# Two attention layers on one core: value products for 512 queries, output products in one step behind the value transposes

## The chip, the core and the metric

The kernel runs on one core of a Trainium2 chip. The metric is the device time of one execution in microseconds; for each kernel the median of several runs is given. The profile is that of one execution, taken by the hardware profiler; its times are in microseconds unless marked ns. Its engines are PE (TensorE's matmuls), PEld (TensorE's weight loads), DVE (VectorE), ACT (ScalarE), POOL (GpSimd) and SP (SyncE, which here issues most DMAs).

## The reference

Two layers of the same form run over an input of 4 images of 32 x 32 positions and 768 channels, all in float32. Each layer adds to its input an attention over the group-normalised input. With 12 heads of 64 channels and 1024 positions:

```python
qkv = x @ Wqkv                                   # layer 1 also adds a bias
q, k, v = ...                                    # (B * 12, 1024, 64) each
rel_h = jnp.einsum('bhwc,hkc->bhwk', r_q, Rh)    # relative positions, rows
rel_w = jnp.einsum('bhwc,wkc->bhwk', r_q, Rw)    # and columns
bias = rel_h[..., :, None] + rel_w[..., None, :]
scores = scale * jnp.einsum('bqc,bkc->bqk', q, k) + bias
attn = jax.nn.softmax(scores, axis=-1)
out = jnp.einsum('bqk,bkc->bqc', attn, v)
return out @ Wproj + bproj
```

## The kernel before

**Units of work.** The 2 layers x 4 images are 8 images in a row. The 12 heads of an image are taken in 6 pairs, one head on partitions 0 to 63 and the other on 64 to 127, so there are 48 pairs, `g`. The 1024 queries of a pair are taken in 8 tiles of 128. One `(g, n)` is a unit, and the main loop (line 520) makes one step for each. The eight steps of a pair are called a slot below, its steps 0 to 7.

**What a step does**, in the order in which it is written. The order on each engine is the order of the program. `run(early)` issues what earlier steps put off: DMAs, relative positions, statistics. What a function puts into `early` runs in the next step, what it puts into `later` runs two steps on (one step on, if it was put there while `run(early)` ran). `biases` (two GpSimd additions, line 303) prepares the unit two ahead. `scores` computes the unit one ahead: 4 matmuls on PE (line 315), two DVE reductions that add the bias and take the minimum of the negated scores (line 324), two exps on ACT (line 328). `turn` transposes the present unit's weights on DVE in blocks of 32 (line 352), and for every second unit, that is for each quarter of 256 queries, writes them to memory (`td`, line 355), from where `read_back` (line 361) brings them back as `pt` with the keys on the partitions. `divide` takes reciprocals of the sums on DVE (line 335) and multiplies on GpSimd (line 338). `take(todo, n)` runs n units of pending PE work, `weigh` the product of weights and values.

**Pending PE work.** `todo` holds for each slot six input groups of the next pair (`project_in`, line 222: q, k and v, each in two halves, 6 units of two matmuls each), and behind them four output groups (`project_out`, line 437, usually 3 units of one matmul each) of the image. An input group ends with an ACT copy (lines 232 or 234) and a DVE addition (line 235), an output group with a DVE addition (446 or 449), and in layer 0 with statistics of the new image (line 149). `shares` says how many units each step takes: 6 in every step, as a rule. In steps with an even number, a first output group is taken ahead of `turn`, so that its eviction isn't queued behind the transposes on DVE.

**Values.** When an input group of v is complete, `late` gets `turn_values` (line 247): 8 transposes on PE (line 252) and one ACT copy (line 253). It runs at the end of a step, behind `weigh`. `weigh` (line 366) runs in every even step for one quarter of 256 queries: 16 matmuls (line 373) and a DVE copy (line 378).

**Shapes on the array.** Scores, positions and inputs contract over 64 rows and fill 128 columns, two at a time in the two halves of the array (64*128 in the profile). `weigh` contracts over 128 rows with 64 columns (128*64). Outputs and value transposes use the whole array (128*128).

**Buffers.** PSUM holds two pools of two buffers: `ps_s` for scores, and `ps_m` for all else (inputs, positions, value transposes, value products, outputs), whose two buffers are taken in turn. `tb` has three buffers, `pt` two for each head, `td` two for each head.

**Image boundaries.** The next image is normalised in stages: statistics (`load_stats`, `stats`), exchange over groups of channels (`norm`: gather, by_group, groups, spread, in steps 1, 3, 5, 7 of pair 3), and `apply` for each of six tiles (line 197): three in steps 2 to 4 of pair 4, three in step 0 of pair 5, ahead of the input groups that read them.

Of the kernel before, what the change touches and what calls it, by code (L numbers as in the profile page):

```python
# [31 lines left out]
FP = mybir.dt.float32  # L32
# [4 lines left out]
P = 128  # L37
B, HW, C = 4, 32, 768
S = HW * HW
# [15 lines left out]
def attention_blocks(ctx: ExitStack, tc: tile.TileContext, a: dict, out: bass.AP):  # L55
# [284 lines left out]
    def turn(g, n):  # L340

        quarter, j = divmod(n, 2)
        for h in range(2):
            if j == 0:
                tb_of[h] = tbpool.tile([P, HW, 2, HW], FP, tag="tb", name=f"tb_{g}_{n}_{h}")  # L350
            tb = tb_of[h]
            nc.vector.transpose(tb[:, :, j, :], sc_of[g, n, h])  # L352
            if j == 1:
                td = dram2.tile([P, S * 2], FP, tag=f"td{h}", name=f"td_{g}_{n}_{h}")
                nc.sync.dma_start(out=td, in_=tb.rearrange("p k n i -> p (k n i)"))
                behind.append(lambda queue=None, h=h, td=td: read_back(g, quarter, h, td, queue))

    def read_back(g, quarter, h, td, queue=None):
        pt = ptpool.tile([P, 4, NT, 2 * HW], FP, tag=f"pt{h}", name=f"pt_{g}_{quarter}_{h}")
        pt_of[g, quarter, h] = pt  # L360
        (queue or nc.sync).dma_start(
            out=pt.rearrange("p r k t -> p r (k t)"),
            in_=td.rearrange("(r j) (y t) -> (j y) r t", r=4, y=4),
        )

    def weigh(g, quarter):
        if quarter == 0:
            attn_of[g] = apool.tile([P, S], FP, tag="attn", name=f"attn_{g}")
        av = ps_m.tile([P, S], FP, tag="m", name=f"av_{g}_{quarter}")[:, : 2 * P]
        for k in range(NT):  # L370
            for h in range(2):
                rows = slice(h * D, (h + 1) * D)
                nc.tensor.matmul(  # L373
                    av[rows, :], lhsT=v_of[g][:, k, rows], rhs=pt_of[g, quarter, h][:, :, k, :],
                    start=(k == 0), stop=(k == NT - 1),
                )
        at = quarter * 2 * P
        nc.vector.tensor_copy(  # L378
            attn_of[g][:, at : at + 2 * P].rearrange("p (n r i) -> p r n i", n=2, r=4),
            av.rearrange("p (r n i) -> p r n i", n=2, r=4),  # L380
        )


# [46 lines left out]
    def project_out(im, p, o, i):  # L430
        l, b = images[im]
        rows = slice(o * P, (o + 1) * P)
        cols = slice(i * HALF, (i + 1) * HALF)
        c0, c1 = cuts(im)[p : p + 2]
        t = ps_m.tile([P, S], FP, tag="m", name=f"o_{im}_{p}_{o}_{i}")[:, :HALF]
        for c in range(c0, c1):
            nc.tensor.matmul(  # L437
                t, lhsT=wo_of[im, o, c], rhs=attn_of[im * NP + c][:, cols],
                start=(c == c0), stop=(c == c1 - 1),
            )  # L440
# [12 lines left out]
        if at_end:  # L453
            if p == 2:
                nc.sync.dma_start(out=dst[rows, cols], in_=res)
        else:
            early.append(lambda: nc.sync.dma_start(out=dst[rows, cols], in_=res))
        if i == 1 and p < 2:
            early.append(lambda: fetch(place[im, p, o, i] + 4))
        yield True  # L460

    early, mid, later, late, behind = [], [], [], [], []

    def run(todo):
        while todo:
# [9 lines left out]
    def at_outputs(groups):  # L479

        return groups[0][1] if groups and groups[0][1] <= NC // 2 else 0

    def take(groups, n):

        while groups and n > 0:
            group, count = groups[0]
            if next(group, None) is None:
                groups.pop(0)
            else:
                groups[0] = (group, count - 1)  # L490
                n -= 1
        while groups and groups[0][1] == 0:
            for _ in groups.pop(0)[0]:
                pass

    with tc.manual_schedule(engines=ENGINES):
        for c in range(NC):
            for i in range(2):
                stats(0, c, i, xn_of[0][c][:, i * HALF : (i + 1) * HALF])
        stages, apply = norm(0)  # L500
        for stage in stages:
            stage()
        for c in range(NC):
            apply(c)
        todo = prepare(0)
# [12 lines left out]

        units = [(g, n) for g in range(NPAIR) for n in range(NT)]
        for at, (g, n) in enumerate(units):  # L520
            im, pair = divmod(g, NP)
            end = im + 1 == NI
            if n == 0:
                shares = [NC] * NT
                ins = (todo if at == 0 else []) + (prepare(g + 1) if g + 1 < NPAIR else [])
                if pair < 3:
                    if im == 0:
                        shares = [NC if pair == 0 or n != 2 else 0 for n in range(NT)]
                        shares[6] = 0
                    todo = ins + (put_out(im - 1, 1, range(4 * pair, 4 * pair + 4)) if im else [])  # L530
                elif pair < NP - 1:
                    todo = ins + put_out(im, 0, range(4 * pair - 12, 4 * pair - 8))
                    if pair == 3 and not end:
                        stages, apply = norm(im + 1)
                else:
                    todo = ins + put_out(im, 0, range(8, 12))
                    if end:
                        fetch_last()
                        todo += put_out(im, 1, range(12)) + put_out(im, 2, range(0, 12, 2))
                        shares = [6, 3, 3, 4, 2, 4, 2, 6]  # L540
            if pair < 3 and not end and n % 4 == 0 and 2 * pair + n // 4 < AHEAD:
                load_x(im + 1, 2 * pair + n // 4)
            if pair < 3 and im + 1 < B and n % 2 == 0:
                c, i = divmod(4 * pair + n // 2, 2)
                load_stats(im + 1, (c + AHEAD) % NC, i)
            run(early)
            early, later = later, early
            if at + 2 < len(units):
                biases(*units[at + 2])
            if at + 1 < len(units):  # L550
                scores(*units[at + 1])
            ready = late[:1]
            del late[:1]
            ready_reads = list(behind)
            behind.clear()
            if pair == 3 and n % 2 and not end:
                stages[n // 2]()
            if pair == 4 and n in range(2, 2 + AHEAD) and not end:
                apply(n - 2)
            if pair == NP - 1 and n == 0 and not end:  # L560
                for c in range(AHEAD, NC):
                    apply(c)
            share = shares[n]
            first = min(share, at_outputs(todo)) if n % 2 == 0 else 0
            take(todo, first)
            turn(g, n)
            run(ready_reads)
            if at + 1 < len(units):
                divide(*units[at + 1])
            take(todo, share - first)  # L570
            if n % 2 == 0 and at > 3:
                weigh(units[at - 4][0], units[at - 4][1] // 2)
            run(ready)
        for read in behind:
            read(nc.scalar)
        weigh(NPAIR - 1, 2)
        while todo:
            take(todo, 1)
            run(early)
        weigh(NPAIR - 1, 3)  # L580
        todo = put_out(NI - 1, 2, range(1, 12, 2))
        take(todo, len(todo))

# [46 lines left out]
```

## Time and profile before

| | |
|---|---|
| time, median of 3 runs | 3642.38 us (3632.63 to 3643.9) |
| span of the profiled execution | 3635.1 us |
| granted TensorE clock | 0.997 |
| memory traffic | 1090.59 MB, 300 GB/s in the mean |
| DMA engines, main queue | 81.6% of 16 engines' time |
| write of the weights (`td<-tb`) | 384 of 1024 KB, 7.3 us to landing |
| read of the weights (`pt<-td`) | 384 of 1024 KB, 7.5 us to landing |

How to read it: in the profile's first part each engine has its busy time, its share of the span and the number of its instructions. In its second part the span is cut into 40 slices, and each digit is the busy share (or the granted clock) in tenths. Groups of instructions are named out<-in by the program's tiles, with the line of the kernel, the count and the mean duration. In a timeline the first two numbers are the start and the duration of a run of like instructions; matmuls are pipelined, so the durations of neighbours overlap and the difference of two starts is the time that the first one took. What stands in brackets is idle time of the engine ahead of the instruction, and who ended it.

### The profile page before, as it was taken

The numbers are of one execution on the slowest core, as the hardware profiler recorded it, in microseconds if no ns is written. First come the engines' busy times: TensorE is split into PE (matmuls) and PEld (weight loads), VectorE is DVE, ScalarE is ACT, GpSimd is POOL, SyncE is SP. The second block draws the span as 40 slices with busy tenths as digits, with TensorE's granted clock in tenths as the row PEclk, the third lists the DMA queues.
The fourth block names the chain that finished last, engine by engine and source line by source line (L and its number), as shares of the span: only waits on it lengthen the run. The fifth ranks groups of instructions, "written<-read, shape, count | busy, mean of one in ns | idle before, by whom it ended". The sixth has DMA issues, their size and how long they took to land.

```text
span 3635.1 us, 51496 instructions
## 1 busy us (share of the span) xinstructions
PE 3558.3 (98%) x19200; PEld 1717.1 (47%) x19200; DVE 2380.7 (65%) x3628; ACT 1316.8 (36%) x1992; POOL 2292.4 (63%) x1548
## 2 busy tenths in 40 slices
PE   6999999999999999999999999999999999999998
PEld 3544444444444444444444444444444444444443
DVE  4676666766667666666666666666666666666665
ACT  2344333333333333333333343333333333333331
POOL 3676666666656666666666666666666566666663
PEclk9999999999999999999999999999999999999999
DMA  4888888898888988888888989888888888898888
GB/s 141 298 314 294 313 293 307 297 312 311 293 310 300 312 300 309 316 293 311 307 302 309 313 281 328 303 304 300 300 314 299 311 288 315 297 321 284 304 293 305
DMA packets 632346, 1090.59 MB, mean 300 GB/s; under 512 B 248096, under 2 KB 310304, under 8 KB 582944
## 3 DMA queue, kind: packets, MB, share of 16 engines
q1 hardware_dynamic: 580352, 1034.87, 81.6%
q10 hardware_dynamic: 51744, 52.44, 4.2%
q8 instruction: 151, 2.47, 0.3%
q14 instruction: 99, 0.81, 0.1%
HBM read 583.74 MB, written 503.41 MB: 299 GB/s over the span
## 4 chain that ended last, share of the span: by engine, by line
PE 84%; DMA 9%; DVE 3%; issue 2%; SPq 1%; POOL 1%; ACT 0%; DVEq 0%; POOLq 0%
PE pj L222 36%; PE s L315 17%; PE av L373 17%; PE o L437 11%; DMA td<-tb 4%; PE tp L267 2%; DMA pt<-td 2%; PE vt L252 1%; DVE sc L324 1%; DVE tb L352 1%; POOL sc L338 1%; SPq L293 1%; DMA xs<-in_x 1%; DMA part<-res 1%; DMA w<-in_wqkv 0%
## 5 line engine op out<-in xcount | busy, mean ns | idle before, releaser
L338 POOL TENSOR_SCALAR sc<-sc,sm 128x1024 f32<-128x1024 f32 x768 | 849.3, 1118 | 1246.9 <-DVE sm L335 1215.7
L222 PE MATMUL pj<-xn,w 64*128 64x512 f32 x6912 | 1541.4, 591 | 40.1 <-DVE xn L197 38.0
L303 POOL TENSOR_TENSOR sc<-rel 128x1024 f32<-128x1024 f32 x768 | 1454.0, 1914 | 45.0 <-DMA rel<-tdr 45.0
L328 ACT ACTIVATE sc<-sc,sm 128x1024 f32<-128x1024 f32 x768 | 879.0, 1145 | 1366.4 <-DVE sm L324 1366.4
L324 DVE CUSTOM_DVE_ANT_0 sc<-s,sc 128x1024 f32<-128x1024 f32 x768 | 909.5, 1222 | 479.0 <-PE s L315 403.4
L222 PEld LDWEIGHTS pj<-xn,w 64*128 64x128 f32 x6912 | 673.6, 188 | 858.4 <-issue 799.5
L352 DVE STREAM_TRANSPOSE tb<-sc 128x1024 f32<-128x1024 f32 x768 | 918.6, 1225 | 149.0 <-DMA td<-tb 147.1
L315 PE MATMUL s<-k,q 64*128 64x512 f32 x3072 | 751.4, 605 | 6.2 <-DVE sm L324 6.2
L373 PE MATMUL av<-pt,v 128*64 128x256 f32 x6144 | 715.0, 384 | 12.4 <-DMA pt<-td 12.4
L373 PEld LDWEIGHTS av<-pt,v 128*64 128x64 f32 x6144 | 427.5, 137 | 358.3 <-issue 76.1
L437 PE MATMUL o<-attn,wo 128*128 128x512 f32 x1128 | 510.8, 601 | 4.3 <-DVE sum L449 2.7
L315 PEld LDWEIGHTS s<-k,q 64*128 64x128 f32 x3072 | 276.9, 187 | 316.8 <-issue 267.5
L437 PEld LDWEIGHTS o<-attn,wo 128*128 128x128 f32 x1128 | 206.0, 190 | 301.7 <-issue 291.4
L378 DVE COPY attn<-av 128x256 f32<-128x256 f32 x192 | 80.9, 422 | 283.3 <-PE av L373 283.1
L235 DVE TENSOR_TENSOR v<-pj,v 128x512 f32<-128x512 f32 x96 | 107.5, 1120 | 132.1 <-ACT v L234 70.2
L272 ACT COPY t<-tp 128x1024 f32<-128x1024 f32 x96 | 97.1, 1012 | 206.3 <-PE tp L267 205.3
L253 ACT COPY v<-vt 128x1024 f32<-128x1024 f32 x48 | 48.6, 1012 | 262.0 <-PE vt L252 262.0
L328 ACT ACTIVATION_READ_ACCUMULATOR sc<-sc,sm 128x1 f32 x768 | 143.4, 187 | 0.0
L267 PEld LDWEIGHTS tp<-tab,q 64*128 64x128 f32 x1536 | 97.5, 187 | 47.0 <-issue 38.6
L235 DVE TENSOR_TENSOR q<-pj,q 128x512 f32<-128x512 f32 x96 | 65.7, 685 | 72.7 <-ACT q L232 37.3
L235 DVE TENSOR_TENSOR k<-pj,k 128x512 f32<-128x512 f32 x96 | 65.7, 685 | 71.2 <-ACT k L232 39.9
L267 PE MATMUL tp<-tab,q 64*128 64x128 f32 x1536 | 106.3, 278 | 5.3 <-DVE k L235 5.3
(38 smaller groups left out, 755.3 us busy)
## 6 DMA issues: line engine op xcount, KB each, us to landing
td<-tb SPq DMA_DIRECT2D x384, 1024.0 KB, 7.3
pt<-td SPq DMA_DIRECT2D x382, 1024.0 KB, 7.5
w<-in_wqkv SPq DMA_DIRECT2D x144, 384.0 KB, 8.5
tdr<-t ACTq DMA_DIRECT2D x96, 512.0 KB, 7.5
rel<-tdr SPq DMA_DIRECT2D x768, 32.0 KB, 2.3
part<-res SPq DMA_DIRECT2D x96, 256.0 KB, 8.3
res<-part SPq DMA_DIRECT2D x96, 256.0 KB, 3.2
wo<-in_wo SPq DMA_DIRECT2D x90, 192.0 KB, 7.5
```

The lines of the kernel that those rows point to most:

```text
L222: nc.tensor.matmul(t[:, a, :], lhsT=w[rows, c, :], rhs=xn[c][rows, cols], start=(c == 0), stop=(c == NC - 1),)
L235: nc.vector.tensor_tensor(to, t[1], to, ALU.add)
L267: nc.tensor.matmul(ps[:, h, j, :], lhsT=q[rows, at * P : (at + 1) * P], rhs=tabs[l][rows, :], start=True, stop=True,)
L272: nc.scalar.copy(t, ps.rearrange("p h j r -> p j h r"))
L303: nc.gpsimd.tensor_tensor(sc, rel[:, h, 0, n, :].unsqueeze(2).to_broadcast([P, HW, HW]), rel[:, h, 1, n, :].unsqueeze(1).to_broadcast([P, ...
L315: nc.tensor.matmul(ps[h][:, cols], lhsT=q[rows, n * P : (n + 1) * P], rhs=k[rows, cols], start=True, stop=True,)
L324: nc.vector.tensor_tensor_reduce(out=sc, in0=ps[h], in1=sc, scale=-scale, scalar=BIG, op0=ALU.add, op1=ALU.min, accum_out=st[:, 0, h : h + 1],
L328: nc.scalar.activation(sc, sc, AF.Exp, bias=st[:, 0, h : h + 1], scale=-1.0, accum_out=st[:, 1, h : h + 1],)
L338: nc.gpsimd.tensor_scalar(sc, sc, st[:, 2, h : h + 1], 1.0, ALU.mult, ALU.mult)
L352: nc.vector.transpose(tb[:, :, j, :], sc_of[g, n, h])
L373: nc.tensor.matmul(av[rows, :], lhsT=v_of[g][:, k, rows], rhs=pt_of[g, quarter, h][:, :, k, :], start=(k == 0), stop=(k == NT - 1),)
L437: nc.tensor.matmul(t, lhsT=wo_of[im, o, c], rhs=attn_of[im * NP + c][:, cols], start=(c == c0), stop=(c == c1 - 1),)
```

## The change

The change sorts PE's work by the shape in which it uses the array, so that the shape changes less often in a slot:

- `weigh` takes two quarters at once (512 queries[...]) and runs in step 6 for the first two quarters of the pair, in step 2 of the next slot for the other two. Nothing else but scores (and positions) runs on PE in these steps.
- All four output groups run in step 7, and `turn_values` moves from the end of a step to just ahead of them, right behind the scores of step 7.
- Input groups run in steps 0, 1, 3, 4 (two) and 5.
- The read-back of the first and third quarter is put off by a step (`behind2`), the loads for the output groups too (`later`), the statistics and stages move to other steps, and the next image's tiles are applied in steps 2, 6 and 7 of pair 4, four of them between the first and second output group.
- In the last slot the shares differ, and the last two quarters are weighed one by one.

```diff
-                behind.append(lambda queue=None, h=h, td=td: read_back(g, quarter, h, td, queue))
+                (behind if quarter % 2 else behind2).append(
+                    lambda queue=None, h=h, td=td: read_back(g, quarter, h, td, queue)
+                )
...
-    def weigh(g, quarter):
-        if quarter == 0:
+    def weigh(g, quarters):
+        if quarters[0] == 0:
...
+        for at, quarter in enumerate(quarters):
+            for k in range(NT):
+                for h in range(2):
+                    rows = slice(h * D, (h + 1) * D)
+                    nc.tensor.matmul(
+                        av[rows, at * 2 * P : (at + 1) * 2 * P], lhsT=v_of[g][:, k, rows],
+                        rhs=pt_of[g, quarter, h][:, :, k, :], start=(k == 0), stop=(k == NT - 1),
+                    )
...
-            early.append(lambda: fetch(place[im, p, o, i] + 4))
+            (early if im + 1 == NI else later).append(lambda: fetch(place[im, p, o, i] + 4))
...
-                shares = [NC] * NT
+                shares = [6, 6, 0, 6, 12, 6, 0, 12]
...
-                    if im == 0:
-                        shares = [NC if pair == 0 or n != 2 else 0 for n in range(NT)]
-                        shares[6] = 0
+                    if at == 0:
+                        shares = [12, 6, 0, 6, 12, 6, 0, 0]
...
-                        shares = [6, 3, 3, 4, 2, 4, 2, 6]
+                        shares = [0, 6, 6, 4, 2, 2, 0, 8]
...
-            if pair < 3 and im + 1 < B and n % 2 == 0:
+            if pair < 3 and im + 1 < B and n in (1, 3, 5, 6):
...
             if at + 1 < len(units):
                 scores(*units[at + 1])
-            ready = late[:1]
-            del late[:1]
-            ready_reads = list(behind)
-            behind.clear()
-            if pair == 3 and n % 2 and not end:
-                stages[n // 2]()
-            if pair == 4 and n in range(2, 2 + AHEAD) and not end:
-                apply(n - 2)
-            if pair == NP - 1 and n == 0 and not end:
-                for c in range(AHEAD, NC):
-                    apply(c)
-            share = shares[n]
-            first = min(share, at_outputs(todo)) if n % 2 == 0 else 0
-            take(todo, first)
+            if late and n == NT - 1 or at == 1:
+                late.pop(0)()
+            run(behind)
+            behind, behind2 = behind2, behind
+            if pair == 3 and n in (1, 3, 6, 7) and not end:
+                stages[(1, 3, 6, 7).index(n)]()
+            if pair == 4 and n in (2, 6) and not end:
+                apply(n // 4)
             turn(g, n)
-            run(ready_reads)
             if at + 1 < len(units):
                 divide(*units[at + 1])
-            take(todo, share - first)
-            if n % 2 == 0 and at > 3:
-                weigh(units[at - 4][0], units[at - 4][1] // 2)
-            run(ready)
+            share = shares[n]
+            if pair == 4 and n == 7 and not end:
+                take(todo, 3)
+                share -= 3
+                for c in range(2, NC):
+                    apply(c)
+            take(todo, share)
+            if n == 6:
+                weigh(g, (0, 1))
+            elif n == 2 and g:
+                weigh(g - 1, (2, 3))
...
-        weigh(NPAIR - 1, 2)
+        weigh(NPAIR - 1, (2,))
         while todo:
             take(todo, 1)
             run(early)
-        weigh(NPAIR - 1, 3)
+            run(later)
+        weigh(NPAIR - 1, (3,))
```

More of the change, by code (lines that the diff above doesn't have):

```diff
@@ L364, in read_back @@
         )
-    def weigh(g, quarter):
-        if quarter == 0:
+    def weigh(g, quarters):
+        if quarters[0] == 0:
             attn_of[g] = apool.tile([P, S], FP, tag="attn", name=f"attn_{g}")
[L369 to L377, printed above, removed]
+        n = len(quarters)
+        av = ps_m.tile([P, S], FP, tag="m", name=f"av_{g}_{quarters[0]}")[:, : n * 2 * P]
+        for at, quarter in enumerate(quarters):
[6 more added lines that the diff above has]
+                    )
+        at = quarters[0] * 2 * P
         nc.vector.tensor_copy(
-            attn_of[g][:, at : at + 2 * P].rearrange("p (n r i) -> p r n i", n=2, r=4),
-            av.rearrange("p (r n i) -> p r n i", n=2, r=4),
+            attn_of[g][:, at : at + n * 2 * P].rearrange("p (q n r i) -> p q r n i", q=n, n=2, r=4),
+            av.rearrange("p (q r n i) -> p q r n i", q=n, n=2, r=4),
         )
@@ L458, in project_out @@
         if i == 1 and p < 2:
-            early.append(lambda: fetch(place[im, p, o, i] + 4))
+            (early if im + 1 == NI else later).append(lambda: fetch(place[im, p, o, i] + 4))
         yield True
-    early, mid, later, late, behind = [], [], [], [], []
+    early, mid, later, late, behind, behind2 = [], [], [], [], [], []
     def run(todo):
@@ L477, in put_out @@
         return [(project_out(im, p, at // 2, at % 2), c1 - c0) for at in groups]
-    def at_outputs(groups):
-        return groups[0][1] if groups and groups[0][1] <= NC // 2 else 0
     def take(groups, n):
@@ L551, in attention_blocks @@
                 scores(*units[at + 1])
[L552 to L565 removed]
+            if late and n == NT - 1 or at == 1:
[6 more added lines that the diff above has]
+                apply(n // 4)
             turn(g, n)
[L567 removed]
             if at + 1 < len(units):
                 divide(*units[at + 1])
[L570 to L574 removed]
+            share = shares[n]
[9 more added lines that the diff above has]
+                weigh(g - 1, (2, 3))
+        run(behind)
+        run(early)
+        run(later)
+        for read in behind2:
             read(nc.scalar)
[L576 removed]
+        weigh(NPAIR - 1, (2,))
         while todo:
@@ L579, in attention_blocks @@
             run(early)
-        weigh(NPAIR - 1, 3)
+            run(later)
+        weigh(NPAIR - 1, (3,))
         todo = put_out(NI - 1, 2, range(1, 12, 2))
```

## The prediction

> **What bounds the kernel now.** I read the page first: busy shares, granted clock and chain of waits.
>
> ```profile
> PE 3558.3 (98%) x19200; PEld 1717.1 (47%) x19200; DVE 2380.7 (65%) x3628; ACT 1316.8 (36%) x1992; POOL 2292.4 (63%) x1548
> ...
> PEclk9999999999999999999999999999999999999999
> ...
> PE 84%; DMA 9%; DVE 3%; issue 2%; SPq 1%; POOL 1%; ACT 0%; DVEq 0%; POOLq 0%
> ```
>
> PE is busy nearly always, at full clock, and has 84% of the chain; the next engine has a third of its time free. So a change counts by what it does to PE's stream. Next the table of who waited for whom, for PE:
>
> ```profile
> PE pj L222 <- DVE xn L197: 38.0, 8, 26.3
> PE av L373 <- DMA pt<-td: 12.4, 9, 2.3
> ```
>
> 26.3 of the 38.0 us are the start; the other seven waits (about 1.7 us each) fall where a new image begins. All other waits of PE sum to 22.5 us. So busy PE time must hold the cost, and a busy mean cannot show gaps inside it. I read PE's timeline of an undisturbed stretch (start, duration, line, operation, count; one float32 matmul is two records):
>
> ```profile
> 1494.28 5.32 PE L222 MATMUL pj<-xn,w 64*128 64x512 f32 x24
> 1499.43 1.88 PE L315 MATMUL s<-k,q 64*128 64x512 f32 x8
> 1501.15 5.32 PE L222 MATMUL pj<-xn,w 64*128 64x512 f32 x24
> 1506.40 3.67 PE L373 MATMUL av<-pt,v 128*64 128x256 f32 x32
> 1510.00 1.99 PE L315 MATMUL s<-k,q 64*128 64x512 f32 x8
> 1511.82 5.32 PE L222 MATMUL pj<-xn,w 64*128 64x512 f32 x24
> 1516.97 1.88 PE L315 MATMUL s<-k,q 64*128 64x512 f32 x8
> 1518.79 5.42 PE L437 MATMUL o<-attn,wo 128*128 128x512 f32 x12
> 1524.13 3.67 PE L373 MATMUL av<-pt,v 128*64 128x256 f32 x32
> 1527.74 1.09 PE L252 MATMUL vt<-ident,v 128*128 128x128 f32 x8
> 1528.76 1.99 PE L315 MATMUL s<-k,q 64*128 64x512 f32 x8
> 1530.68 5.42 PE L437 MATMUL o<-attn,wo 128*128 128x512 f32 x12
> ```
>
> Read differences of starts. The column after MATMUL gives the array shape: s, pj and tp use 64*128, av 128*64, vt and o 128*128. Scores between two groups of their own shape take 1.72 us (1499.43 to 1501.15). Entered from av and left to pj they take 1.82, entered from pj and left to o 1.82, entered from vt and left to o 1.92. So **a change of shape costs about 0.10 us when leaving and 0.10 when entering**. An input group takes 5.15 inside its shape and 5.25 before av. For av the entry is 0.05 (its pitch of 0.216 us x 16 pairs is 3.45; 3.60 - 3.45 - 0.10 is left), for vt 0.05.
>
> The period: the score matmuls at 1481.00 recur at 1554.56, so a slot (one pair of heads, eight steps) takes 73.56 us, and most do to 0.1 us. Start times of the scores split the span: 58.3 us to the first score matmul, 273.3 for slots 0 to 3, 43 slots in 3196.8, and 106.8 after 3528.35. 43 x 73.56 is 3163.1, so 33.7 us are waits in those slots: seven image boundaries of 1.9 (13.3), and 20.4 elsewhere.
>
> [...] copies stand on ACT in program order.[...] waits of 1 to 2 us leave PEclk at 9 here.
>
> **The change, part by part.**
>
> Shape changes. Before, a slot has 12: pj to av three times, o to av, av to s twice, av to tp, av to vt, vt to s, s to o twice, o to s. Leaving: 12 x 0.097 = 1.16. Entering: five into 64*128 and two into o at 0.10, four into av and one into vt at 0.05: 0.95. Together 2.11. After: steps 0, 1, 3, 4, 5 hold only scores, positions and inputs, steps 2 and 6 scores then av, step 7 scores, vt, outputs. That is 6 changes: 0.58, and three entries into 64*128, two into av, one into vt: 0.45, together 1.03. **Saved: 1.08 us a slot.** vt to o keeps the shape; no row shows that neighbour, so 0 to 0.10, taken as 0.
>
> The new wait. Pool ps_m has two buffers. In step 7 vt takes one, the first output group the other (free: its old content, av of step 6, is copied out by DVE within 0.9 us of the step's start, one 512-wide DVE operation being 0.69). The second output group needs vt's buffer, freed by the ACT copy of line 253. Before, that copy was issued ahead of the next scores' exps and ran at once. After, turn_values follows scores in program order, so the copy is queued behind both exps. Their timing after the scores' start at 1528.76:
>
> ```profile
> 1530.89 1.22 DVE L324 CUSTOM_DVE_ANT_0 sc<-s,sc 128x1024 f32<-128x1024 f32 x1 [2.61 <-PE s L315]
> ```
> ```profile
> 1528.87 1.01 ACT L253 COPY v<-vt 128x1024 f32<-128x1024 f32 x1 [5.87 <-PE vt L252]
> ...
> 1532.22 1.15 ACT L328 ACTIVATE sc<-sc,sm 128x1024 f32<-128x1024 f32 x1 [2.34 <-DVE sm L324]
> ...
> 1533.37 1.13 ACT L328 ACTIVATE sc<-sc,sm 128x1024 f32<-128x1024 f32 x1
> ```
>
> Let T be the start of step 7's scores. DVE's first reduction starts at T+2.13, the second exp at T+4.61; exps follow each other at 1.15, so ACT reaches the copy at T+5.76 and ends it at T+6.77; PE resumes some 0.05 later, T+6.82. PE itself: scores 1.92 with both changes, vt 0.93, first group 6 x 0.429 = 2.57: ready at T+5.42. **It waits 1.40**, and the restart pays the 0.10 entry again (it does after each wait for DVE in the tail: first matmul 0.53 instead of 0.43): 1.50 a slot. Ends: 1.3, if vt to o costs, and some 3, if DVE is late (below). Queued behind it on PE: three output groups and the next scores, so it is on the path in full. Third and fourth group wait for nothing: their evictions are due by T+7.7 and T+10.3, the groups at T+9.5 and T+12.1.
>
> A slot becomes 73.56 - 1.08 + 1.50 = 73.98.
>
> Image boundaries. Normalising (line 197, 1.04 us each) moves ahead of the inputs that need it, so the seven 1.9 us go. Four applies now stand on DVE ahead of the second output eviction, whose buffer the fourth group needs: T+7.6 + 4.2 + 0.7 = T+12.5 against T+12.0, 0.6 x 7 = 4.
>
> Other waits (20.4). They come from DVE waiting for a tb buffer (147.1 us in 77 waits for the td write) while an eviction that PE needs is queued behind. After, evictions needed soon no longer stand behind such a wait: the even steps, where tb is taken, are 7 to 12 us long. The quarter written in step 3 is read from about T4+11 and lands 7.5 later, near 7 us into step 5, needed 12 us in. I keep 6: statistics in the first pair of images 1 and 2 wait on xs and push the exps of step 7 by 2 us, twice, and 2 for jams.
>
> Free: the av copy (one of 512 for two of 256), later fetches (buffers are due a slot later), read-backs two steps on (six microseconds of slack or more). GpSimd needs 6.1 us a step (two at 1.91, two at 1.12), and the shortest steady step is 6.9.
>
> Slots 0 to 3. Without outputs, work is 62.2 a slot: 71.44 less 10.3 of outputs, plus 1.03. Step 7 holds only scores and vt, so the next scores wait for the reductions, about 1.5. Slot 0 has six more input units but two av groups fewer and keeps its start waits, 67; slots 1 to 3: 66 (xs), 64, 64. About 260 against 273; part of this are 5 us of outputs moved into the tail.
>
> Tail. PE work rises to some 89 us (60 output units, 6 av groups, 8 scores) but the outputs stand where scores, divides and transposes had made PE wait (18 us before). Followed step by step with 2.4 us each of reductions and transposes and 7.5 us for each of write and read, the last read lands 87 us in and PE ends at 100; 4.5 for the last eviction and store: 105.
>
> Sum: 58.3 + 260 + 43 x 73.98 (3181) + 4 + 6 + 105 = 3614, 21 under the span of 3635.1. Taken from the median of 3642.4: **3621**.
>
> **Rivals.**
> - *The wait is twice as long.* In step 6 the second transpose needs the tb buffer whose write was issued in step 5. With a landing of 7.4 us (the median) DVE is free over 1 us before step 7; with 12 (the largest is 15.0) it reaches the reductions 1.8 us late, and exps, copy and PE with it. For it: DMA engines are 86% busy. Against: little else is in transit then. Half of the slots so, or all by 1 us: + 43, 3664, slower.
> - *The wait does not come*, the copy running ahead of the exps: 3621 - 43 x 1.5 = 3557. For it: vt is done at T+2.85, ACT idle until T+3.46.[...]
> - *The scattered waits stay* in other places (reads late for the 512-query groups, stops at image starts): 3621 + 20 = 3641, no change.
>
> **How the numbers follow.** Forecast 0.55, longer wait 0.17, no wait 0.12, waits stay 0.16. The forecast carries 12 us either way (the wait 0.15 x 43 = 6, first slots and tail 6 each, scattered waits 5). The range leaves out the no-wait case and the upper part of the longer wait: 3590 to 3664. Faster by over 11 us: 0.47 of the forecast's 0.55, and 0.12; same: 0.08 and 0.11; slower: 0.17 and 0.05.
>
> **What would show it.** Six shape changes a slot; in PE's waits a new line, o L437 for ACT v L253, some 44 times at 1.4; the xn line down to its start; slots of 74.0. I am wrong if that line is missing (then far faster), if its mean is over 2.5 (slower), or if av waits for pt in most slots.

## The result and the profile after

The changed kernel takes **3668.53 us** (median of 4 runs, 3663.02 to 3673.1) where the kernel before took 3641.05 beside it: a ratio of 1.0079, 95% interval 1.0057 to 1.0101. It is slower, and it lies outside the range of the prediction.

The page of the changed kernel, first and second part and chain of waits:

```profile
PE 3530.5 (96%) x19200; PEld 1739.5 (47%) x19200; DVE 2401.9 (66%) x3533; ACT 1309.5 (36%) x1992; POOL 2298.0 (63%) x1548
...
PEclk9999999999999999999999999999999999999999
...
PE 88%; ACT 4%; DVE 3%; DMA 2%; issue 2%; SPq 0%; POOL 0%; DVEq 0%; ACTq 0%; POOLq 0%
```

PE is busy for 28 us less than before (3558.3) in a span that is 32 us longer. That fits fewer changes of shape (the experiments price them), and PE now stands still for longer. ACT is new in the chain, with 4%. The mean granted clock is 0.993 (before 0.997); the row of nines hides that. PE's waits (what waited, for what, us in total, times, longest) say for whom it stands still:

```profile
PE o L442 <- ACT v L253: 44.2, 37, 1.5
PE o L442 <- DVE res L451: 39.9, 14, 3.3
PE pj L222 <- DVE xn L197: 25.9, 1, 25.9
PE o L442 <- DVE sum L454: 9.1, 2, 8.1
PE s L315 <- DVE sm L324: 8.3, 8, 2.3
```

The first line is the wait that was forecast. The third has shrunk to the start of the kernel, as forecast. The second line (14 waits, two in each of seven images) and the fourth (the end of the kernel) are new, and no step of the prediction has them at that size.

The starts of the score matmuls give the balance, by the division that the prediction used (us):

| | before | forecast | after |
|---|---|---|---|
| to the first score matmul | 58.3 | 58.3 | 57.5 |
| slots 0 to 3 | 273.3 | 260 | 261.3 |
| an ordinary slot | 73.56 | 73.98 | 73.93 |
| 43 slots, beyond 43 ordinary ones | 33.7 | 10 | 48.4 |
| tail | 106.8 | 105 | 120.5 |
| span | 3635.1 | 3614 | 3666.7 |

**The ordinary slot** came out to 0.05 us. Its step 7 on PE, then on ACT (start, duration, line, operation, count; in brackets idle time and who ended it):

```profile
1522.30 1.99 PE L315 MATMUL s<-k,q 64*128 64x512 f32 x8
1524.22 1.09 PE L252 MATMUL vt<-ident,v 128*128 128x128 f32 x8
1525.15 2.74 PE L442 MATMUL o<-attn,wo 128*128 128x512 f32 x6
1529.08 7.99 PE L442 MATMUL o<-attn,wo 128*128 128x512 f32 x18 [1.19 <-ACT v L253]
1537.00 1.99 PE L315 MATMUL s<-k,q 64*128 64x512 f32 x8
```
```profile
1526.90 1.13 ACT L328 ACTIVATE sc<-sc,sm 128x1024 f32<-128x1024 f32 x1
...
1528.03 0.99 ACT L253 COPY v<-vt 128x1024 f32<-128x1024 f32 x1
```

The transposes end at 1525.3, but the copy that frees their buffer comes out of ACT's queue behind the second exp, at 1528.03, and PE's second output group starts when it is done, at 1529.08. That is T+6.78, where T is the start of the scores; T+6.82 was forecast.

**The slot of pair 3** in each image takes 75.2 or 76.9 us. The same step there, on ACT and on PE:

```profile
772.52 1.28 ACT L328 ACT_TABLE_LOAD   x1 [4.62 <-DVE sm L324]
773.82 1.15 ACT L328 ACTIVATE sc<-sc,sm 128x1024 f32<-128x1024 f32 x1
...
776.09 0.99 ACT L253 COPY v<-vt 128x1024 f32<-128x1024 f32 x1
```
```profile
771.93 2.74 PE L442 MATMUL o<-attn,wo 128*128 128x512 f32 x6
777.11 9.69 PE L442 MATMUL o<-attn,wo 128*128 128x512 f32 x18 [2.44 <-DVE res L451]
```

The stage with the square root ran in step 5 and now runs in step 6. So a table load of 1.28 us stands ahead of the exps of step 7, where the kernel before had it ahead of those of step 6 (at 772.68 there, its end 2.59 us ahead of the exp). Here the load does not use the 4.62 us for which ACT stood idle: the exp starts 0.02 us behind its end, and the copy comes 1.3 us later than elsewhere. The trace names DVE, whose first eviction ends at 777.05 (its reciprocal waits for the late exps), but the copy that the group needs ends at 777.08: what is late is the queue of ACT. The 18 matmul records behind it take 9.69 us instead of 7.99: in this stretch the granted clock is halved for 3.4 us (778.39 to 781.80). That happens in four of the seven pair-3 slots, and makes the difference between 75.2 and 76.9.

**The slot of pair 4** takes 77.5 or 80.2 us. PE, then DVE:

```profile
848.79 2.74 PE L442 MATMUL o<-attn,wo 128*128 128x512 f32 x6
852.72 5.42 PE L442 MATMUL o<-attn,wo 128*128 128x512 f32 x12 [1.19 <-ACT v L253]
861.40 5.49 PE L442 MATMUL o<-attn,wo 128*128 128x512 f32 x6 [3.27 <-DVE res L451]
```
```profile
852.70 0.73 DVE L451 SCALAR_TENSOR_TENSOR res<-o,bo,res 128x512 f32<-128x512 f32 x1
853.34 7.35 DVE L197 TENSOR_SCALAR xn<-xn,nrm 128x1024 f32<-128x1024 f32 x4
860.61 1.40 DVE L451 SCALAR_TENSOR_TENSOR res<-o,bo,res 128x512 f32<-128x512 f32 x2
```

All applies of the kernel before (shortest, median, longest, ns):

```profile
L197 DVE TENSOR_SCALAR xn<-xn,nrm x48: 800/810/1770, 25.4 to 3098.8; 128x1024 f32<-128x1024 f32 x48
```

The four applies now take 7.35 us, not 4.2, and the fourth output group waits 3.3 us for the eviction behind them. Its six matmul records take 5.49 us instead of 2.7: here too the clock is halved (860.31 to 867.13), in three of the seven images. The granted clock of this stretch (start and end, length, PE's busy time, granted clock, DMA share and GB/s):

```profile
857.00:869.00 12.00, 8.73 (x19) 0.72 0.39 154
```

A mean of 0.72 over 12 us is some 6.7 us at half clock (the clock's record has 6.83), twice as long as in pair 3.

**The tail.** SyncE's queue, then PE:

```profile
3628.88 2.81 SPq L363 DMA_DIRECT2D pt<-td  x2
...
3632.33 2.61 SPq L423 DMA_DIRECT2D res<-part  x4
```
```profile
3641.74 5.59 PE L442 MATMUL o<-attn,wo 128*128 128x512 f32 x8 [8.07 <-DVE sum L454]
```

The writes of `td` were issued at 3620.04 and 3621.17; the read-backs of the last quarter, which wait for them, stand on SyncE's queue at 3628.88 and 3631.32, and the loads of the partial sums (`res<-part`) are queued behind them, at 3632.33. An output group on PE waits 8.07 us, until the DVE addition that takes these loads.

### The profile page after: what moved, and what is told of

Same layout as the page of the kernel before. It is cut to its first block, busy times and chain, and to the rows that moved or that the text cites. A ratio compares the mean times of both kernels' runs of the same rounds, so it can differ in the third digit from the quotient of the medians.

```text
span 3666.7 us, 51253 instructions
## 1 busy us (share of the span) xinstructions
PE 3530.5 (96%) x19200; PEld 1739.5 (47%) x19200; DVE 2401.9 (66%) x3533; ACT 1309.5 (36%) x1992; POOL 2298.0 (63%) x1548
## 4 chain that ended last, share of the span: by engine, by line
PE 88%; ACT 4%; DVE 3%; DMA 2%; issue 2%; SPq 0%; POOL 0%; DVEq 0%; ACTq 0%; POOLq 0%
PE pj L222 40%; PE s L315 18%; PE av L378 17%; PE o L442 10%; ACT sc L328 3%; PE tp L267 3%; DVE xn L197 1%; ACT v L253 1%; DVE sc L324 1%; DVE res L451 0%; DMA pt<-td 0%; DMA xs<-in_x 0%; DVE tb L352 0%; DMA w<-in_wqkv 0%; DMA part<-res 0%
## 5 line engine op out<-in xcount | busy, mean ns | idle before, releaser
L378 PE MATMUL av<-pt,v 128*64 128x256 f32 x6144 | 687.8, 381 | 3.4 <-DVE res L451 3.1
L442 PE MATMUL o<-attn,wo 128*128 128x512 f32 x1128 | 524.0, 614 | 93.3 <-ACT v L253 44.2
L315 PEld LDWEIGHTS s<-k,q 64*128 64x128 f32 x3072 | 289.3, 187 | 342.9 <-issue 321.7
L383 DVE COPY attn<-av 128x512 f32<-128x512 f32 (+1 forms) x97 | 66.2, 683 | 165.0 <-PE av L378 165.0
L451 DVE SCALAR_TENSOR_TENSOR res<-o,bo,res 128x512 f32<-128x512 f32 x96 | 70.7, 744 | 129.4 <-PE o L442 127.6
L454 DVE TENSOR_TENSOR res<-o,res 128x512 f32<-128x512 f32 x84 | 57.6, 686 | 96.8 <-PE o L442 96.8
```

The lines of the kernel that those rows point to most:

```text
L315: nc.tensor.matmul(ps[h][:, cols], lhsT=q[rows, n * P : (n + 1) * P], rhs=k[rows, cols], start=True, stop=True,)
L378: nc.tensor.matmul(av[rows, at * 2 * P : (at + 1) * 2 * P], lhsT=v_of[g][:, k, rows], rhs=pt_of[g, quarter, h][:, :, k, :], start=(k == 0) ...
L442: nc.tensor.matmul(t, lhsT=wo_of[im, o, c], rhs=attn_of[im * NP + c][:, cols], start=(c == c0), stop=(c == c1 - 1),)
```

## The experiments

Every edit is made on the changed kernel, unless it says otherwise. Line numbers in the experiments' profiles are shifted by the lines that an edit adds. The theory to be tested: four separate costs make up the loss, the copy behind the exps in 43 slots, the square root's stage in step 6, the four applies in one block, and the order on SyncE's queue in the tail. Each of the first four experiments takes one away. Each experiment ran beside runs of the kernel before, whose medians lie between 3636 and 3642 us in the four sessions; so a difference in us from the changed kernel is uncertain by a few us.

### The copy ahead of the exps

```diff
+    def exps(g, n):
+        st = st_of[g, n]
+        for h in range(2):
+            sc = sc_of[g, n, h].rearrange("p y x -> p (y x)")
             nc.scalar.activation(
...
             if late and n == NT - 1 or at == 1:
                 late.pop(0)()
+            if at + 1 < len(units):
+                exps(*units[at + 1])
```

> The changed kernel, with the two exps of each unit written behind turn_values, so that in step 7 the copy of line 253 stands ahead of them on ACT; PE's order is untouched. Theory (the copy is late because it is queued behind the exps): the second output group starts at T+5.4 instead of T+6.8, a slot falls from 73.93 to 72.5 us; 29 ordinary slots give 1.45 each, 7 slots with an activation table load in front of the exps 2.7 each and some 5 us of lowered clock, the 7 slots with four normalisations on DVE give nothing (their fourth group waits for DVE anyway): about 3602 us, 1.1% under the kernel before. Rival (PE only meets the next wait, the first group's eviction behind the transposes on DVE, ready at about T+7.8): the third group waits instead, the slot stays at 73.5 or more, 3655 to 3665 us.

Measured: 3616.64 us, 0.9922 of before (0.9907 to 0.9937). The line of waits for ACT's copy is gone, and an ordinary slot takes 72.5 us, as expected; so the wait cost 1.45 us a slot. The time was missed by 14 us. One reason is seen in pair 4:

```profile
839.30 7.89 PE L447 MATMUL o<-attn,wo 128*128 128x512 f32 x18
851.91 5.15 PE L447 MATMUL o<-attn,wo 128*128 128x512 f32 x6 [4.72 <-DVE res L456]
```

PE arrives at the fourth group earlier and waits there for 4.7 us instead of 3.3, and the clock is then halved in all seven images (78.9 to 80.4 us a slot). What was taken from one wait was given to the next, and the seven pair-4 slots take 7 us more in sum than in the changed kernel. A second reason is pair 3, whose slots take 73.2 us, 0.8 more than ordinary ones. The table load (1.28 us in the changed kernel) now stands behind the copy, but it still delays the exps, the reciprocal that needs their sums, and behind it on DVE the first eviction, for which the third output group waits. The rest lies in the first slots (264 instead of 261) and in the tail (121.7).

### One apply behind each output group

```diff
-                take(todo, 3)
-                share -= 3
                 for c in range(2, NC):
+                    take(todo, 3)
+                    share -= 3
                     apply(c)
```

> The changed kernel, with the four normalisations of step 7 of pair 4 set one behind each output group's eviction instead of all four behind the first. Theory (they take 7.35 us on DVE instead of 4.2, since they alternate with GpSimd, and the second eviction stands behind them): the fourth group's wait of 3.4 us and the half clock that follows it in three of seven cases go, 7 x 3.4 + 3 x 2.8 = 32 us less than the changed kernel: about 3636 us. Single normalisations still last 0.8 us alone and up to 2.4 beside GpSimd. Rival (DVE has no room between groups: 2.4 + 0.75 is more than a group's 2.57): each group waits 0.5, 3645 to 3655 us.

Measured: 3639.42 us, 0.9991 of before (0.9984 to 0.9999), 29 less than the changed kernel. Pair-4 slots are ordinary ones, 73.9. The applies in the profile of pair 4's step 7 still take 0.8 to 1.7 us each, but nothing stands behind them that PE needs.

### The last read-backs on ACT's queue

```diff
-        run(behind)
         run(early)
         run(later)
-        for read in behind2:
+        for read in behind + behind2:
             read(nc.scalar)
```

> The changed kernel, with the read-backs of the last quarter issued from ACT's queue, behind the pending loads, as the kernel before did. Theory (the reads wait on SyncE's queue for the write to land, and the loads for the last output groups stand behind them, so that DVE and then PE wait some 8 us for res): the wait of 8.1 us in the last slot falls to under 2, and the half clock behind it goes: 8 to 10 us less than the changed kernel, about 3659 us. Rival (the loads are late because they are issued two steps on): nothing changes, 3668 us.

Measured: 3664.23 us, 1.0052 of before (1.0037 to 1.0067). The tail takes 112.3 us instead of 120.5, and the wait of 8.1 becomes 1.0. The medians show 4 of these 8 us, and the intervals of the two ratios overlap, so it is the traces that show the effect. In this run's profile the first four slots took 266 us, in the changed kernel's 261, with the same program there. The edit takes the reads off SyncE's queue and also puts them behind the loads in the program; which of the two would be enough was not tried.

### The square root's stage back in step 5

```diff
-            if pair == 3 and n in (1, 3, 6, 7) and not end:
-                stages[(1, 3, 6, 7).index(n)]()
+            if pair == 3 and n in (1, 3, 5, 7) and not end:
+                stages[(1, 3, 5, 7).index(n)]()
```

> The changed kernel, with the third stage of the next image's normalisation (the one with the square root on ACT) back in step 5, the others as they are. Theory (the table that the exps need is loaded again only when the first exp of the next step is due, 1.28 us, and in step 7 exps, copy and second output group stand behind it): the seven waits of 2.4 us fall to 1.2, and the half clock that followed in three of them goes: 7 x 1.25 + 3 x 1.7 = 14 us less than the changed kernel, about 3654 us. Rival (the wait is longer there because DVE is late from the stage's small operations): it stays, 3668 us.

Measured: 3651.83 us, 1.0029 of before (1.0021 to 1.0038). Pair-3 slots take 73.9, without half clock, and the wait for ACT's copy is counted 44 times instead of 37, as the prediction had it. Pair-4 slots are all at 77.5 in this profile, none at 80.2. Their wait is 3.3 us as before, but no window of the clock got more than 1.93 us of it (see the last section); this part of the gain, some 8 us in the profile, is luck and not the edit's.

### The value transposes in step 6

Another way to take the copy from behind the exps: the transposes run at the end of step 6, behind the value products, at the price of a change of shape.

```diff
-            if late and n == NT - 1 or at == 1:
+            if at == 1:
                 late.pop(0)()
...
                 weigh(g, (0, 1))
+                if late:
+                    late.pop(0)()
```

> The changed kernel, with turn_values at the end of step 6, behind the value products, where the copy stands on ACT ahead of the exps; PE now goes av, vt, scores, outputs, which is one more change of shape in a slot. Theory: the wait of 1.45 us goes as it does with the copy ahead of the exps, and the added change costs 0.2: an ordinary slot takes 72.7 us (72.5 with the copy ahead), 29 x 1.25 + 7 x 2.5 + 5 + 1 = 60 us less than the changed kernel, about 3608 us. Rival (a change of shape costs nothing where the next weights are ready): 72.5 us a slot.

Measured: 3647.99 us, 1.0025 of before (1.0017 to 1.0034). A miss: 40 us above the expectation. An ordinary slot takes 73.1 us, not 72.7. PE's waits and step 7 on PE:

```profile
PE o L442 <- DVE res L451: 43.6, 30, 5.1
```
```profile
1517.53 1.99 PE L315 MATMUL s<-k,q 64*128 64x512 f32 x8
1519.44 10.97 PE L442 MATMUL o<-attn,wo 128*128 128x512 f32 x24
```

24 matmul records at 0.429 us are 10.3 us; here the next scores start after 10.91. The outputs now stand right behind the scores, so their third group is due 0.9 us earlier, before DVE has done the transposes of `turn` and evicted the first group. The transposes on PE had been filling that time. In 29 slots that makes 12 us. The largest part of the miss, some 15 us, is pair 4, where the same shift makes the wait 5.1 us, with half clock in every image (80.1 to 81.2 us a slot). Pair-3 slots, at 73.6 us, and the first slots (266 us) add some 7 and 5.

### All four together

The edits of the first four experiments in one kernel.

> The changed kernel with four edits together: the copy of line 253 ahead of the exps, the normalisations one behind each output group, the last read-backs on ACT's queue, the stage with the square root in step 5. Theory (the four waits are all that lies between the work and the span): 57.5 to the first scores, some 266 for slots 0 to 3, 43 slots of 72.5 with no longer ones among them (3118), some 111 for the tail: a span near 3552, a time of about 3555 us, 2.4% under the kernel before. Rival (PE's waits move on to DVE's evictions once the copy is early, or DMA becomes the bound with 2.3% less time for the same bytes): slots of 73 or more, 3575 us or more.

Measured: **3551.07 us, 0.9757 of before (0.9742 to 0.9773)**. It beats both kernels. All 43 slots take 72.5 us, those of pairs 3 and 4 included. The first four of PE's waits:

```profile
PE pj L222 <- DVE xn L197: 26.4, 1, 26.4
PE s L315 <- DVE sm L324: 9.8, 8, 2.5
PE av L383 <- DVE res L456: 4.6, 1, 4.6
PE o L447 <- DVE sum L459: 0.9, 1, 0.9
```

Nothing but the start, the first slots and the tail is left. The four edits gave 52, 29, 4 and 17 us alone (102 in sum) and 117 together. By the ratios to the kernel before the four sum to 117 as well, so the times show no gain beyond the sum; in the traces the longer wait that the first edit alone left in pair 4 is gone. The slot gives the price of the shapes: 73.56 before less 72.46 (43 slots in 3115.9) is 1.10 us for the six changes saved; 1.08 was forecast.

### Quarters again

The kernel with all four edits, with value products for 256 queries in steps 2, 3, 5 and 6: four more changes of shape in a slot, all else equal.

> The kernel with the four edits, but with value products for 256 queries again: the third and fourth quarter in steps 2 and 3 of the next slot, the first and second in steps 5 and 6 (in the last slot as before). That adds four changes of shape to a slot, two from inputs to av at 0.15 and two from av to scores at 0.20, and nothing else on PE. Theory (a change of shape costs what the timeline before shows): a slot takes 72.5 + 0.70 = 73.2 us, 45 x 0.7 = 31 us more than with the four edits: about 3586 us. Rival (it is the grouping of evictions, not the shape, that saves): the slot stays at 72.5, within 5 us of the kernel with the four edits.

Measured: 3583.11 us, 0.9847 of before (0.9831 to 0.9862). An ordinary slot takes 73.17 us, 0.70 more than with all four edits (72.46), as expected: 0.18 for a change of shape. (Seven slots, one in each of seven images, take 73.42.) The rival, that only the grouping of evictions saves, is out.

### The shares of the last slot

The kernel with all four edits, with the shares of the kernel before in the last slot.

> The kernel with the four edits, and with the last slot's shares as in the kernel before (6, 3, 3, 4, 2, 4, 2, 6 instead of 0, 6, 6, 4, 2, 2, 0, 8). Theory (with no output unit in step 0 PE waits for the reductions, and with six in step 2 the value products wait for an eviction behind DVE's transposes; both showed in the changed kernel's tail): 3 to 6 us less than with the four edits, about 3550 us. Rival (the tail is set by the last write and read of the weights, 17 us in any order): no difference.

Measured: 3552.02 us, 0.9761 of before (0.9743 to 0.9779): no difference. These two sets of shares give the same time.

### Why the applies took so long: two other forms

In the changed kernel the six applies at the start, with GpSimd idle, take 0.81 us each. Those of step 7 in pair 4 are longer, and how much goes with what GpSimd does beside them: 1.20 us beside a multiplication (line 338), 1.60 between a multiplication and an addition (line 303), 2.39 beside the additions. First, a form of the same operation with two tensor inputs:

```diff
-            nc.vector.tensor_scalar(
-                xn_of[im][c], xn_of[im][c], nrm[:, c, 0:1], nrm[:, c, 1:2], ALU.subtract, ALU.mult
+            nc.vector.scalar_tensor_tensor(
+                xn_of[im][c], xn_of[im][c], nrm[:, c, 0:1], nrm[:, c, 1:2].to_broadcast([P, S]),
+                ALU.subtract, ALU.mult,
             )
```

> The changed kernel, with the normalising of a tile (line 197) written as a scalar_tensor_tensor whose second tensor is the reciprocal deviation, broadcast along the row, in place of a tensor_scalar: the same values, but an operation with two tensor inputs. Theory (the four applies of step 7 in pair 4 took 7.35 us[...]): the new form runs [...]as the transposes of 1024 elements do (1.22 us), whatever GpSimd does, so the four take about 4.8 us instead of 7.35, all of equal length. The fourth output group then waits 3.3 - 2.5 = 0.8 us, pair-4 slots take 73.9 + 0.8 = 74.7 instead of 77.5 or 80.2, and half clock goes there: 7 x 2.5 and 3 x 2.8, 26 us less than the changed kernel, about 3642. Rival[...]: the new form is lengthened as well, to 1.6 to 2.8 us each beside the additions, the sum stays at 7 us or more, pair-4 slots stay at 77.5 and above, time 3665 to 3675.

Measured: 3694.99 us, 1.0157 of before (1.0126 to 1.0189). The expectation failed. All applies of this kernel (shortest, median, longest, ns), and GpSimd beside the four of pair 4:

```profile
L197 DVE SCALAR_TENSOR_TENSOR xn<-xn,nrm x48: 1280/2133/2926, 25.7 to 3136.8; 128x1024 f32<-128x1024 f32 x48
```
```profile
863.38 5.71 POOL L304 TENSOR_TENSOR sc<-rel 128x1024 f32<-128x1024 f32 x2
```

In the changed kernel the same two additions:

```profile
855.49 4.65 POOL L303 TENSOR_TENSOR sc<-rel 128x1024 f32<-128x1024 f32 x2
```

The form is slower alone (1.28 us) and is lengthened just the same; the four take 9.5 us, more than the rival had said. GpSimd is lengthened too: its two additions take 5.71 us here, 4.65 in the changed kernel, and 3.78 beside DVE's reductions and transposes (at 848.45 there). An apply that is 0.47 us longer by itself makes each addition beside it 0.53 longer. What lengthens the two, no trace shows.

So the form with two tensor inputs was no way out. The other form is a `tensor_scalar` that also writes an accumulator, which nothing reads:

```diff
+            acc = small.tile([P, 1], FP, tag="acc", name=f"acc_{im}_{c}")
             nc.vector.tensor_scalar(
-                xn_of[im][c], xn_of[im][c], nrm[:, c, 0:1], nrm[:, c, 1:2], ALU.subtract, ALU.mult
+                xn_of[im][c], xn_of[im][c], nrm[:, c, 0:1], nrm[:, c, 1:2], ALU.subtract, ALU.mult,
+                accum_out=acc,
```

> The changed kernel, with the normalising of a tile (line 197) kept as a tensor_scalar but given an accumulator output, which nothing reads.[...] Theory[...]: [...]the new form takes 1.2 to 1.3 us with its accumulator read 0.1 more, beside GpSimd as well as alone; the four take 5.2 us instead of 7.35, the fourth output group waits 3.3 - 2.1 = 1.2 us, pair-4 slots take 75.1 instead of 77.5 or 80.2, without half clock: 7 x 2.4 and 3 x 2.8, 25 less than the changed kernel, about 3643. GpSimd's additions beside it stay at 1.91 us. Rival[...]: each apply is lengthened by 0.4 to 1.6 us again, the four take 9.7 us as with two tensor inputs, and the time is about 3690.

Measured: 3649.35 us, 1.0025 of before (1.0014 to 1.0037).

```profile
L198 DVE TENSOR_SCALAR_CACHE_REDUCE xn<-xn,nrm x48: 1322/1334/1373, 25.1 to 3094.3; 128x1024 f32<-128x1024 f32 x48
```
```profile
857.17 3.78 POOL L305 TENSOR_TENSOR sc<-rel 128x1024 f32<-128x1024 f32 x2
```

All 48 take 1.32 to 1.37 us, beside GpSimd or alone, and GpSimd's two additions keep their 3.78 (one takes 1.90 to 1.92 us, over all 768). Of the two engines' lengthening nothing is left in this form; why, no trace shows. The four applies take 5.1 us, pair-4 slots 75.2 (75.1 expected), and the clock stays whole there. The time is 6 above the expectation: half clock followed in five of the seven pair-3 slots instead of four (1.7 us), and slots 0 to 3 took 265 us (3.5).

## Why the prediction was wrong

Its likeliest case said 3621; the sum for the span missed by 53 us. By its own steps:

- **Shape changes: right.** 1.08 us a slot forecast, 1.10 measured with all four edits; 0.15 to 0.20 a change forecast, 0.18 measured with the quarters. From transposes to outputs, which keep the shape, the median excess over 44 cases is 0.0, so the 0 taken there was right.
- **The new wait: right.** 1.50 us forecast; the slot without it is 73.93 - 72.46 = 1.47 shorter. The copy came behind both exps on ACT, as the program has them (1526.90 and 1528.03 above), and that was all that it took. Neither rival to it came: none of the 37 is over 1.5, and none is missing (the other seven, in pair 3, are counted to DVE).
- **Image boundaries: wrong, and by most.** The seven waits of 1.9 us went, as said. The step "Four applies now stand on DVE ahead of the second output eviction" was right in its mechanism; the term that was mis-sized is 4 x 1.04. That mean comes from a group whose members had very different neighbours: before, the shortest took 800 ns, the median 810 and the longest 1770. In the new place they run beside GpSimd's two multiplications and two additions, and take 7.35. T+7.6 + 7.35 + 0.7 is T+15.6; the group started at T+15.45. The wait is 3.3 us, and costs 3.5 a slot, not 0.6 (the prediction's own T+12.5 and T+12.0 give 0.5).
- **The stages: a step that was missing.** The prediction put the moved stages at nothing, without naming what would hide them. The table load ahead of the exps, 1.28 us, hit the step in which the new wait stands behind them. 7 x 1.28 is 9 us.
- **The clock: wrong.** The forecast had no half clock in it. Its reading that waits of 1 to 2 us leave PEclk at 9 says little, since a digit of that row is the mean of 91 us: the trace before has 3.4 us of half clock at 591.7, behind a wait of 1.96 us (`av` for `pt`, ended at 591.04). In the changed kernel half clock followed waits of 2.4 us in four of seven cases, at 1.7 each (7 us), and after the waits of pair 4 in three of seven, at 2.75 (8 us). With the two items above, 7 x 3.5 + 9 + 7 + 8 is 48.5; 48.4 was measured beyond the ordinary slots, 10 forecast.
- **Scattered waits: right.** DVE's wait for the write of `td` fell from 147.1 us to 7.9, and one wait of `av` for `pt` is left, of 0.3 us. The 6 us kept for such waits did not come.
- **First slots: right**, 261.3 for 260; the profiles of the second to fourth experiments have 261 to 266 there.
- **Tail: wrong.** The step "followed step by step" counted the landing times of writes and reads, and not that the loads written behind the waiting reads stand behind them on SyncE's queue (the reads issued at 3628.88 and 3631.32, the loads from 3632.33). That is 8 us of the 15.5, shown by the third experiment. Of the rest, the last slot's shares are not the cause. Waits in the last slot, some of them for a DVE eviction, and half clock after them are seen; which of them sets the 110.8 us that remain with all four edits wasn't tried.
- The forecast also added the 7 us by which the median of before stood over its profiled span. The changed kernel's median stands 1.8 over its span, so this made the miss look smaller.

## What to carry to other kernels

When work is gathered into one step, list all that stands in that step on every engine's queue, stages that come once in an image as well: a wait that is harmless in 41 slots of 48 can be the longest in the other seven. Take the duration of an operation that is moved from the row of its new neighbours (its shortest and its longest, not the mean of its group), and for VectorE ask whether GpSimd runs beside it (an apply took 0.81 us alone and 2.39 beside GpSimd's additions). And once a wait has been removed, look at once for the next one in the same step, since PE merely arrives there sooner.

## What the runs showed of the hardware

- **Half clock followed windows with some 2 us of idle PE.** The traces record the granted clock, and in each of the twelve every change of it lies on one beat of 3.413 us. For slots 4 to 46 of all twelve, the idle time of PE in each window between two beats tells the clock of the next. After a window at full clock with up to 1.94 us of idle PE the clock stayed full (11079 windows), after one with 1.96 us or more it was halved (53). In the kernel before, the two values nearest to this border are 1.66 (full) and 1.96 (halved), in the changed kernel 1.88 and 2.03. A window at half clock was followed by another where PE had been idle in it for 0.78 us or more (23), and by full clock up to 0.53 us (53). So **in these traces the share of a wait that fell into one window told the clock, not the length of the wait**. The same wait of 3.3 us in pair 4 brought 6.8 us of half clock where 2.2 us of it lay in one window, and none where the larger part was 1.7 to 1.9; in the fourth experiment no window got more than 1.93, and the clock stayed full in all seven images. In the first slots and the tails five windows with 1.3 to 1.8 us were followed by half clock too (in the kernel before one with 1.72, ahead of 62.60); why less was enough there wasn't tried.
- **A table load waited with its exp in one kernel, and not in the other.** In the changed kernel the seven table loads ahead of the exps of step 7 took 1.28 us each, and the exp started up to 0.02 later; so 1.30 is what one costs on the path. They began only when the exp's own wait was over, though ACT had been idle for 4.61 to 4.77 us. In the kernel before, the same loads stood behind a copy, began 0.02 us after its end, and ended 2.5 to 2.6 us ahead of the exp: there they cost nothing on the path. What decides between the two wasn't tried.
- **Both engines were lengthened.** Where applies and additions alternate, one of either takes about the same time, and that is the sum of the two alone less some 0.3 us: 2.39 and 2.35 us in the changed kernel (0.81 and 1.91 alone), 2.93 and 2.89 with two tensor inputs (1.28 and 1.91 alone).
